# A recurrent chain of four layers: when the preparation for the last layers is done, and in which pieces

## The chip, the cores and the metric

The kernel runs on one NeuronCore of a Trainium2 chip. The metric is the device time of one execution in microseconds (us), the median of several runs. A NeuronCore has a matrix engine (TensorE, in profiles PE, its weight loads PEld), two engines for elementwise work (VectorE or DVE, ScalarE or ACT), a programmable one (GpSimd or POOL) and a synchronisation engine (SyncE or SP) that issues most DMA transfers here. Each engine takes its own instructions strictly in the order in which the program gives them, and they wait for each other through semaphores. TensorE writes to PSUM[...]; the other engines read results from there.

## The reference

Four residual layers follow one another on x of shape (4, 1024, 512), with a conditioning vector per batch row:

```
x = x + rnn(x)            # h = tanh(x_t Wx + h Wh), 1024 steps in order
x = x + ssm(x)            # convolution, projections, a scan with decay, projection
x = x + lstm(x)           # gates = x_t Wx2 + h Wh2, 1024 steps in order
x = x + adaptive(x, cond) # x @ layer[b]; layer[b] = base + A_b B_b^T
```

`A_b` and `B_b` (512 by 8 each) come from the conditioning vector: layer norm, a hidden layer with Gelu, and a product with the big matrix w2. They don't depend on x, so they are prepared while the recurrences run. Everything is in fp32; the LSTM's recurrent product is done with three bf16 parts of Wh2 and three of h.

## The kernel before

Time is cut into 32 chunks of 32 steps (`TC`, `NCHUNK`). The RNN runs `LEAD` = 56 steps ahead of the LSTM. `do_pass(c)` is one chunk of LSTM steps, with the RNN steps 56 further on; the passes c = -2 (24 steps) and c = -1 (32 steps) have RNN steps alone and are called the lead here. Its steps are counted 0 to 55; step 24 is the first of pass -1. One RNN step is 16 matrix products on TensorE (`rnn_mm`, line 337, 32 records since an fp32 product is two instructions), a transpose and an addition on VectorE (`rnn_pre`, lines 352 and 353) and a tanh on ScalarE (`rnn_h`, line 356). One LSTM step is 96 products (line 369) in two halves A and Bh, each followed by a transpose, a sum, gates, products, cell, tanh, h and two splits of h.

The order of every engine's instructions is written out by hand (`manual_schedule`). Within a step there are three places for other work: "pe", after the LSTM's products and ahead of the RNN's; "gap", ahead of the tanh of half Bh; and "end", after the RNN's tanh. Jobs of a chunk (`ssm_jobs`, `input_jobs`, `project0`, `adapt_jobs`) are lists of (step, place, function). In chunk 0 there is no adaptive layer of an earlier chunk, so that the "pe" place of steps 17, 19, 21 and 23 is empty; that of 29 and 31 is empty in all chunks. In the lead, `keep_busy` adds eight products without use per step up to step 31.

The preparation is a separate list, `early`: a function registered with `at(c, t, f)` or `at_step(i, f)` (lead step i) runs at the very end of that step. It holds, in this order of steps:

- `split_wh2` (269 to 283): 16 pieces of Wh2 (128 by 512 each), loaded into the later place of `layer`, are split into three bf16 parts. Each piece takes four instructions, alternately on ScalarE and VectorE: part 0 (276), remainder `left` (277), part 1 (280), part 2 (281). The first two of a piece are in one step and the last two in the next, steps 5 to 21.
- `load_w1`, `load_w2`, `load_base` at steps 10, 14 and 18, and 21: SyncE loads into the places of `layer` that the split has read. w2 comes in 32 pieces of 512 KB through four buffers.
- `fold_conv` (20), `adapt_center` (23), `adapt_norm` (25), `adapt_bias` (26, 27), `double_g` (27 to 30, one ScalarE instruction each), `adapt_hidden` (31: 16 products, transpose, addition, Gelu).
- `adapt_w2` (583 to 595): 16 groups of 16 products on two pieces of w2 each, with a copy by ScalarE and the loads of the two pieces that come two groups later. Six groups are in the lead, at steps 35, 38, ... 50, and ten in chunk 0, at steps 1, 3, ... 19.
- `adapt_gather` (597): eight small DMAs from GpSimd for each half, at steps 3 and 19 of chunk 0.
- `base_identity` (628): 16 VectorE additions of 32 by 32 that add twice the identity to the base layer, at step 21 of chunk 0.
- `adapt_sum` (619), at steps 22 and 23.
- `adapt_layer` (622 to 626): 16 times one product of 8 by 128 and 8 by 512 (two TensorE instructions, into a bank of PSUM) and one VectorE addition of 128 by 512, at steps 24 of chunk 0 to 12 of chunk 1. The 8 rows of batch row b lie at partition 32 b.

Banks come from `bank`; the tag "fill" has two and serves the projections, `adapt_w2` and `adapt_layer`, in turn.

For each chunk `adapt_jobs` adds the LSTM's output to x (696), multiplies with `layer` (703), copies the result by ScalarE (710) and writes it out with four DMAs (712), during the next chunk. For the last chunk the same is called after the last step (line 827).

Of the kernel before, what the change touches and what calls it, by code (L numbers as in the profile page):

```python
# [8 lines left out]
F32 = mybir.dt.float32  # L9
BF16 = mybir.dt.bfloat16  # L10
AF = mybir.ActivationFunctionType
ALU = mybir.AluOpType
# [26 lines left out]
def cond_resid_kernel(ctx: ExitStack, tc: tile.TileContext, a: dict, out: bass.AP):  # L39
# [145 lines left out]
    def upper(x):  # L185

        return x.bitcast(BF16)[..., 1::2]
# [81 lines left out]
    def split_wh2(k, g):  # L269

        w, scale, cols = layer[:, k, g], 1.0 if g == 3 else 0.5, slice(g * D, (g + 1) * D)
        part = [x[:, k, cols] for x in wh2]
        left = xw2[1][:, 2 + g % 2].rearrange("p c t b -> p (c t b)")

        def first():
            nc.scalar.activation(part[0], upper(w), AF.Copy, scale=scale)
            nc.vector.scalar_tensor_tensor(left, w, scale, part[0], ALU.mult, ALU.subtract)

        def second():
            nc.scalar.copy(part[1], upper(left))  # L280
            nc.vector.tensor_tensor(part[2], left, part[1], ALU.subtract)

        return first, second


    def bank(name, shape, tag="fill", bufs=2):
        return psum.tile(shape, F32, name=name, tag=tag, bufs=bufs)
# [331 lines left out]
    def adapt_sum(half):  # L619
        nc.vector.tensor_add(turned[half], turned[half], plain(raw[half]))  # L620

    def adapt_layer(b, k):
        r = slice(32 * b, 32 * b + RANK)
        pl = bank("pl", [P, D])
        nc.tensor.matmul(pl, xt[0][r, k * P : (k + 1) * P], xt[1][r], start=True, stop=True)  # L625
        nc.vector.tensor_add(layer[:, b, k, :], base[:, k, :], pl)

    def base_identity():

        for c in range(KC):  # L630
            for j in range(4):
                n0 = P * j + CT * c
                q = slice(CT * j, CT * (j + 1))
                nc.vector.scalar_tensor_tensor(
                    base[q, c, n0 : n0 + CT], ident[q, q], 2.0, base[q, c, n0 : n0 + CT],
                    ALU.mult, ALU.add,
                )


    early = {}  # L640

    def at(c, t, f):
        early.setdefault((c, t), []).append(f)
# [8 lines left out]
    late = None  # L652
    for n in range(4 * KC):
        first, second = split_wh2((1, 0, 2, 3)[n // 4], n % 4)
        if late:
            at_step(5 + n, late)
        at_step(5 + n, first)
        late = second
    at_step(21, late)

    at_step(10, load_w1)
# [4 lines left out]
    at_step(23, adapt_center)  # L666
    at_step(25, adapt_norm)
    for half in range(2):
        at_step(26 + half, lambda half=half: adapt_bias(half))
    at_step(26, lambda: nc.scalar.activation(b2[:, 3], b2[:, 3], AF.Copy, scale=2.0))  # L670
    for k in range(KC):
        at_step(27 + k, lambda k=k: double_g(k))
    at_step(31, adapt_hidden)
    NPRE = 12
    for j in range(0, NW2, 2):
        f = lambda j=j: adapt_w2(j)
        if j < NPRE:
            at_step(35 + 3 * j // 2, f)
        else:
            at(0, j - NPRE + 1, f)  # L680
        if j % (NW2 // 2) == NW2 // 2 - 2:
            at(0, j - NPRE + 1, lambda half=j // (NW2 // 2): adapt_gather(half))
    at(0, 21, base_identity)
    for half in range(2):
        at(0, 22 + half, lambda half=half: adapt_sum(half))
    for n in range(B * KC):
        c, t = divmod(24 + 4 * n // 3, TC)
        at(c, t, lambda n=n: adapt_layer(n % B, n // B))


    def adapt_jobs(c, dst):
        x3 = work.tile([P, KC, B, TC], F32, name="x3", tag="x3")
        ps = bank("ada", [P, D], tag="ada", bufs=1)

        def add(m):
            nc.vector.scalar_tensor_tensor(  # L696
                x3[:, m].rearrange("p b t -> p t b"), h2[c % 2][:, m, :, 0], 0.5, x2[c % 2][:, m],
                ALU.mult, ALU.add,
            )

        def mm(k):
            for b in range(B):
                nc.tensor.matmul(  # L703
                    ps[TC * b : TC * (b + 1), :], x3[:, k, b, :], layer[:, b, k, :],
                    start=(k == 0), stop=(k == KC - 1),
                )

        def end():
            x4 = work.tile([P, D], F32, name="x4", tag="x4")
            nc.scalar.copy(x4, ps)  # L710
            for b in range(B):
                nc.sync.dma_start(out=dst(b), in_=x4[TC * b : TC * (b + 1), :])

        jobs = [((0, 1, 2, 6)[m], ("end", "gap")[m // 3], lambda m=m: add(m)) for m in range(KC)]
        jobs += [(17 + 2 * k, "pe", lambda k=k: mm(k)) for k in range(KC)]
        return jobs + [(23, "end", end)]


    def input_jobs(c, n, steps, turns):
# [14 lines left out]
        ]  # L734


    def do_pass(c, first=0, src=None, dst=None):

        lstm = c >= 0
        jobs = []  # L740
        if dst is not None:
            jobs += adapt_jobs(c - 1, dst)
        if -1 <= c < NCHUNK - 1:
            jobs += ssm_jobs(c + 1)
            jobs += input_jobs(
                c + 1, 0, range(25, 29), ((28, "end"), (29, "gap"), (29, "end"), (30, "gap"))
            )
        if src is not None:
            jobs.append((9, "end", lambda: load_x(c + 4, src)))
        if c + 3 < NCHUNK:  # L750
            for m in range(KC):
                mm, end = project0(c + 3, m)
                t = (18, 20, 22, 30)[m]
                jobs += [(t, "pe", mm), (t, "end", end)]
        if lstm:
# [64 lines left out]
    for c in range(-1, NCHUNK):  # L820
        if c == 0:
            for m in range(2):
                lstm_input(0, 0, m)
        do_pass(c, src=a["xT"][c + 4] if c + 4 < NCHUNK else None, dst=dst(c - 1) if c > 0 else None)
    assert not early
    prep_ctx.close()
    for _, _, f in adapt_jobs(NCHUNK - 1, dst(NCHUNK - 1)):
        f()


# [56 lines left out]
```

## Time and profile before

The median of three runs is 4768.19 us (4766.73 to 4770.69). The profiled execution took 4770.03 us, of which 4768.2 us lie between its first and last instruction (the span); the granted TensorE clock was 0.999 of full speed on average.

| stage | from, to (us of the span) | length |
|---|---|---|
| loads and first projection, to the end of RNN step 0 | 0 to 19.4 | 19.4 |
| lead, steps 1 to 23 | 19.4 to 83.2 | 63.8 |
| lead, steps 24 to 55 | 83.2 to 157.4 | 74.2 |
| chunk 0 | 157.4 to 320.0 | 162.6 |
| chunk 1 | 320.0 to 473.3 | 153.3 |
| chunks 2 to 30 | 473.3 to 4614.8 | 142.8 each on average |
| chunk 31 | 4614.8 to 4757.3 | 142.5 |
| last adaptive layer and end | 4757.3 to 4768.2 | 10.9 |

A step of the lead ends here with the tanh on line 356, an LSTM step with the second addition on line 415. The page gives the busy time and share of each engine, the granted clock and DMA traffic in slices of the span, and the chain of waits: from the last instruction back to what released it, step by step. Groups of instructions have their line, engine, operation, output and inputs, shape and mean duration. Windows give the same busy times for a stretch of the span. In timelines, "[0.79 <-ACT wh L280]" after an instruction means that its engine had been idle for 0.79 us before it, until line 280 on ScalarE was done; "issue" means that it waited for nothing that the profile shows.

### The profile page before, as it was taken

Reading aid. Unit: us, or ns where it says so; the run is one execution under the profiler, and the core shown is the slowest. Engines: PE = TensorE matmul, PEld = TensorE weight load, DVE = VectorE, ACT = ScalarE, POOL = GpSimd, SP = SyncE. Lnnn points to the kernel's source line nnn. Section 1 sums busy time; section 2 is a strip of 40 time slices with the busy share of each in tenths; the row PEclk is TensorE's granted clock in tenths of the full one; section 3 lists DMA queues with packets and bytes.
Section 4 is the critical chain, followed back from the end, with each engine's and each line's share of the span. In section 5 each row is a group of like instructions: output and inputs, shape, how many; then the busy total and the mean of one; then the engine's idle time right before and its main releaser. Section 6 shows DMA issues by size and latency. Waiting matters only on the chain.

```text
span 4768.2 us, 320158 instructions
## 1 busy us (share of the span) xinstructions
PE 4608.4 (97%) x146784; PEld 3524.3 (74%) x146784; DVE 3867.3 (81%) x18001; ACT 1493.9 (31%) x7645; POOL 45.6 (1%) x80
## 2 busy tenths in 40 slices
PE   7999999999999999999999999999999999999976
PEld 5767777777777777777777777777777777777654
DVE  3688888888888888888888888888888888888876
ACT  2223333333333333333333333333333333333322
POOL 3000000000000000000000000000000000000000
PEclk9999999999999999999999999999999999999999
DMA  6300000000000000000000000000000000000000
GB/s 148 112 13 9 9 7 9 9 7 9 9 7 9 9 7 9 9 7 9 9 7 9 9 7 9 9 7 9 9 7 9 9 7 9 9 5 7 6 5 7
DMA packets 38266, 67.36 MB, mean 14 GB/s; under 512 B 8609, under 2 KB 25505, under 8 KB 35889
## 3 DMA queue, kind: packets, MB, share of 16 engines
q1 hardware_dynamic: 34064, 46.68, 3.6%
q8 instruction: 1147, 18.79, 1.6%
q14 instruction: 207, 1.69, 0.1%
q0 software_dynamic: 1696, 0.19, 0.0%
q10 hardware_dynamic: 1152, 0.01, 0.0%
HBM read 38.34 MB, written 8.39 MB: 10 GB/s over the span
## 4 chain that ended last, share of the span: by engine, by line
PE 94%; DVE 4%; DMA 1%; issue 1%; ACT 0%; SPq 0%; ACTq 0%; DVEq 0%
PE acc L369 59%; PE acc L337 18%; PE proj L318 9%; PE pb L292 3%; PE proj L292 2%; PE ada L703 2%; DVE tt L386 1%; DVE gc L391 1%; DVE h L191 1%; PE ssm_out L292 1%; DMA layer<-in_w_dram 1%; DVE h L415 0%; DVE prod L402 0%; DVE gc L407 0%; PE pl L625 0%
## 5 line engine op out<-in xcount | busy, mean ns | idle before, releaser
L369 PE MATMUL acc<-wh,h 128*12 128x256 bf16 x98304 | 2868.0, 273 | 118.4 <-DVE h L191 115.2
L369 PEld LDWEIGHTS <-h 128*12 128x12 bf16 x98304 | 2262.6, 87 | 676.8 <-DVE h L191 360.6
L386 DVE STREAM_TRANSPOSE tt<-acc 128x256 f32<-128x256 f32 x2048 | 920.9, 450 | 429.2 <-PE acc L369 301.4
L337 PEld LDWEIGHTS acc<-wh,h 128*4 128x4 f32 x32768 | 805.4, 87 | 510.0 <-issue 214.8
L337 PE MATMUL acc<-wh,h 128*4 128x128 f32 x32768 | 1086.1, 273 | 18.1 <-ACT h L356 11.0
L398 ACT ACTIVATE gc<-gc 128x32 f32<-128x32 f32 x2048 | 469.8, 229 | 1279.1 <-DVE gc L391 1192.2
L391 DVE TENSOR_REDUCE gc<-tt 128x32 f32<-128x128 f32 x2048 | 775.4, 379 | 35.3
L191 DVE TENSOR_TENSOR h<-h 128x8 f32<-128x8 f32 (+1 forms) x4098 | 680.5, 166 | 104.8
L412 ACT ACTIVATE th<-gc 128x8 f32<-128x8 f32 x2048 | 427.7, 209 | 830.1 <-DVE gc L407 830.1
L356 ACT ACTIVATE h<-pre 128x16 f32<-128x16 f32 x1024 | 221.2, 216 | 1132.2 <-DVE pre L353 1132.2
L318 PE MATMUL proj<-wx,x 128*32 128x512 f32 x4096 | 529.1, 592 | 1.1 <-DVE x L507 1.1
L415 DVE SCALAR_TENSOR_TENSOR h<-gc,th 128x8 f32<-128x8 f32 x2048 | 341.8, 167 | 144.6 <-ACT th L412 134.7
L407 DVE SCALAR_TENSOR_TENSOR gc<-prod 128x8 f32<-128x8 f32 x2048 | 342.0, 167 | 35.5
L352 DVE STREAM_TRANSPOSE tt<-acc 128x128 f32<-128x128 f32 x1024 | 316.0, 309 | 61.8 <-PE acc L337 61.6
L375 ACT COPY tt<-xw 128x32 f32<-128x32 f32 x2048 | 327.8, 207 | 0.0
L402 DVE SCALAR_TENSOR_TENSOR prod<-gc 128x16 f32<-128x16 f32 x2048 | 314.3, 153 | 0.0
L353 DVE TENSOR_TENSOR pre<-xw,tt 128x16 f32<-128x16 f32 x1024 | 179.3, 175 | 38.0 <-DVE tt L352 0.5
L292 PE MATMUL proj<-xin,wx 128*32 128x128 f32 x4096 | 137.9, 278 | 11.1 <-DMA wx<-in_Wx_dram 11.1
L703 PE MATMUL ada<-layer,x 128*32 128x512 f32 x1024 | 133.9, 599 | 3.0 <-DVE x L696 3.0
L292 PE MATMUL pb<-x,wp 128*32 128x128 f32 x4096 | 134.4, 273 | 0.0
L292 PEld LDWEIGHTS proj<-xin,wx 128*32 128x32 f32 x4096 | 117.5, 112 | 14.9 <-DMA wh<-in_Wh_dram 11.1
L318 PEld LDWEIGHTS proj<-wx,x 128*32 128x32 f32 x4096 | 118.3, 110 | 6.6 <-DVE x L507 1.4
(118 smaller groups left out, 1168.8 us busy)
## 6 DMA issues: line engine op xcount, KB each, us to landing
layer<-in_w2T_dram SPq DMA_DIRECT2D x32, 512.0 KB, 4.5
xin<-in_xT_dram SPq DMA_DIRECT2D x128, 64.0 KB, 2.4
out_dram<-x SPq DMA_DIRECT2D x128, 64.0 KB, 2.0
layer<-in_Wh_dram SPq DMA_DIRECT2D x16, 256.0 KB, 9.9
wx<-in_Wx_dram SPq DMA_DIRECT2D x4, 1024.0 KB, 15.6
wx<-in_Wx_dram SPq DMA_DIRECT2D x4, 256.0 KB, 4.6
wh<-in_Wh_dram SPq DMA_DIRECT2D x4, 256.0 KB, 7.2
layer<-in_w_dram SPq DMA_DIRECT2D x4, 256.0 KB, 23.9
```

Source lines behind the costliest of these rows:

```text
L191: nc.vector.tensor_tensor(h[:, :, n], h[:, :, n - 1], upper(h[:, :, n - 1]), ALU.subtract)
L292: nc.tensor.matmul(dst[CT * j : CT * (j + 1)], columns(j), x, start=first, stop=final)
L318: nc.tensor.matmul(ps[CT * j : CT * (j + 1), :], tok, w[:, j], start=(k == 0), stop=(k == KC - 1))
L337: nc.tensor.matmul(acc0[CT * j : CT * j + B, :], h[:, k, (t - 1) % TC, :], wh0[:, k, j * P : (j + 1) * P], start=(k == 0), stop=(k == KC - 1),
L369: nc.tensor.matmul(acc2[mh][CT * j : CT * j + NP * B, :], parts, w[:, :, n0 : n0 + 2 * CT], start=(k == 0 and n == 0), stop=(k == KC - 1 a ...
L375: nc.scalar.copy(tt2[m][t % 2][:, :, :, :B], xw2[c % 2][:, :, 2 * m : 2 * m + 2, t, :])
L386: nc.vector.transpose(self.tt[:, :, :, B:].rearrange("p g c b -> p (g c) b"), acc2[self.m])
L391: nc.vector.tensor_reduce(self.gc[:, :4].rearrange("p g c b -> p (g c) b"), self.tt[:, :, :, : (1 + NP) * B].rearrange("p g c (s b) -> p ( ...
L398: nc.scalar.activation(self.gc[:, :4], self.gc[:, :4], AF.Tanh, scale=0.5)
L407: nc.vector.scalar_tensor_tensor(self.c, self.prod[:, 1], 0.5, self.prod[:, 0], ALU.mult, ALU.add)
L412: nc.scalar.activation(self.th, self.c, AF.Tanh, scale=0.5)
L415: nc.vector.scalar_tensor_tensor(self.out[:, :, 0], self.gc[:, 2], 1.0, self.th, ALU.add, ALU.mult)
```

## The change

1. `split_wh2` gives its four instructions singly, and each is put at its own step: piece i starts at step 5 + i, its four instructions at steps 5 + i, 6 + i, 7 + i and 8 + i. The remainders have four buffers. Within a step the order is: part 2 of piece i - 3 and remainder of piece i - 1 (VectorE), part 1 of piece i - 2 and part 0 of piece i (ScalarE). The last is at step 23. The loads and `adapt_center` that follow move by one or two steps.
2. `adapt_hidden` goes from step 31 to 29, `double_g` to 30, 32, 34 and 36.
3. The w2 groups: eight in the lead (steps 31, 33, 35, 39, 41, 45, 47, 51), eight in chunk 0 (steps 1, 3, ... 15). The first gather is at step 51 of the lead, the second at step 15 of chunk 0; the sums at steps 6 and 18 of chunk 0.
4. The identity is added at steps 40, 42, 44 and 46 of the lead, four additions each.
5. `adapt_layer` does two batch rows at once: two products, one after the other in TensorE's order, then one addition; the second addition is put at the end of the next step (`later`). The pairs are at steps 19, 21, 23, 29 and 31 of chunk 0 and 10, 12 and 14 of chunk 1.
6. In the last chunk, the output for steps 0 to 27 is added to x during steps 28 and 29; after the last step come additions for the four others, and the products in two halves of 256 columns. The first half is copied by ScalarE and written out from SyncE, the second copied by VectorE and written out from ScalarE's queue.

```diff
-        left = xw2[1][:, 2 + g % 2].rearrange("p c t b -> p (c t b)")
+        left = xw2[g % 2][:, 2 + g // 2].rearrange("p c t b -> p (c t b)")
+        return (
+            lambda: nc.scalar.activation(part[0], upper(w), AF.Copy, scale=scale),
+            lambda: nc.vector.scalar_tensor_tensor(left, w, scale, part[0], ALU.mult, ALU.subtract),
+            lambda: nc.scalar.copy(part[1], upper(left)),
+            lambda: nc.vector.tensor_tensor(part[2], left, part[1], ALU.subtract),
+        )
...
-    def adapt_layer(b, k):
-        r = slice(32 * b, 32 * b + RANK)
-        pl = bank("pl", [P, D])
-        nc.tensor.matmul(pl, xt[0][r, k * P : (k + 1) * P], xt[1][r], start=True, stop=True)
-        nc.vector.tensor_add(layer[:, b, k, :], base[:, k, :], pl)
+    def adapt_layer(n):
+        def add(b, k, pl):
+            nc.vector.tensor_add(layer[:, b, k, :], base[:, k, :], pl)
+        pls = []
+        for x in (n, n + 1):
+            b, k = x % B, x // B
+            r = slice(32 * b, 32 * b + RANK)
+            pl = bank("pl", [P, D])
+            nc.tensor.matmul(pl, xt[0][r, k * P : (k + 1) * P], xt[1][r], start=True, stop=True)
+            pls.append((b, k, pl))
+        add(*pls[0])
+        later.append(lambda: add(*pls[1]))
...
+    stages = [split_wh2((1, 0, 2, 3)[n // 4], n % 4) for n in range(4 * KC)]
+    for i in range(4 * KC + 3):
+        for n, f in ((i - 3, 3), (i - 1, 1), (i - 2, 2), (i, 0)):
+            if 0 <= n < 4 * KC:
+                at_step(5 + i, stages[n][f])
+    at_step(11, load_w1)
     for j in range(W2_BUFS):
-        at_step((14, 18)[j // 2], lambda j=j: load_w2(j))
-    at_step(21, load_base)
+        at_step((15, 19)[j // 2], lambda j=j: load_w2(j))
+    at_step(23, load_base)
...
+    at_step(29, adapt_hidden)
     for k in range(KC):
+        at_step(30 + 2 * k, lambda k=k: double_g(k))
+        at_step(40 + 2 * k, lambda k=k: base_identity(k))
+    for j in range(0, NW2 // 2, 2):
+        at_step((31, 33, 35, 39, 41, 45, 47, 51)[j // 2], lambda j=j: adapt_w2(j))
+        at(0, j + 1, lambda j=j: adapt_w2(NW2 // 2 + j))
+    at_step(51, lambda: adapt_gather(0))
+    at(0, NW2 // 2 - 1, lambda: adapt_gather(1))
+    at(0, 6, lambda: adapt_sum(0))
+    at(0, 18, lambda: adapt_sum(1))
+    for n, (c, t) in enumerate(((0, 19), (0, 21), (0, 23), (0, 29), (0, 31), (1, 10), (1, 12), (1, 14))):
+        at(c, t, lambda n=n: adapt_layer(2 * n))
...
+    def last_adapt(c, dst):
+        x3, x4 = adapt_tile("x3"), adapt_tile("x4")
+        ready = TC - 4
+        def rest():
+            for m in range(KC):
+                adapt_add(c, m, x3, ready)
+            for n, (tag, copy, dma) in enumerate(
+                (("ada", nc.scalar.copy, nc.sync), ("po", nc.vector.tensor_copy, nc.scalar))
+            ):
+                cols = slice(n * D // 2, (n + 1) * D // 2)
+                ps = bank("ada", [P, D // 2], tag=tag, bufs=1)
+                for k in range(KC):
+                    adapt_mm(k, x3, ps, cols)
+                copy(x4[:, cols], ps)
+                for b in range(B):
+                    dma.dma_start(out=dst(b)[:, cols], in_=x4[TC * b : TC * (b + 1), cols])
+        return [(28 + m // 2, ("gap", "end")[m % 2], lambda m=m: adapt_add(c, m, x3, 0, ready)) for m in range(KC)], rest
...
             do(t, "end")
+            while later:
+                later.pop()()
             for f in early.pop((c, t), ()):
                 f()
+        if last is not None:
+            rest()
```

More of the change, by code (lines that the diff above doesn't have):

```diff
@@ L272, in split_wh2 @@
         part = [x[:, k, cols] for x in wh2]
-        left = xw2[1][:, 2 + g % 2].rearrange("p c t b -> p (c t b)")
[L275 to L283, printed above, removed]
+        left = xw2[g % 2][:, 2 + g // 2].rearrange("p c t b -> p (c t b)")
[5 more added lines that the diff above has]
+        )
     def bank(name, shape, tag="fill", bufs=2):
@@ L620, in adapt_sum, with base_identity @@
         nc.vector.tensor_add(turned[half], turned[half], plain(raw[half]))
-    def adapt_layer(b, k):
-        r = slice(32 * b, 32 * b + RANK)
-        pl = bank("pl", [P, D])
-        nc.tensor.matmul(pl, xt[0][r, k * P : (k + 1) * P], xt[1][r], start=True, stop=True)
-        nc.vector.tensor_add(layer[:, b, k, :], base[:, k, :], pl)
[L628 to L640, printed above, removed]
+    def adapt_layer(n):
[10 more added lines that the diff above has]
+        later.append(lambda: add(*pls[1]))
+    def base_identity(c):
+        for j in range(4):
+            n0 = P * j + CT * c
+            q = slice(CT * j, CT * (j + 1))
+            nc.vector.scalar_tensor_tensor(
+                base[q, c, n0 : n0 + CT], ident[q, q], 2.0, base[q, c, n0 : n0 + CT],
+                ALU.mult, ALU.add,
+            )
+    early, later = {}, []
     def at(c, t, f):
@@ L651, in cond_resid_kernel @@
         at_step(1 + n // 2, f)
[L652 to L661, printed above, removed]
+    stages = [split_wh2((1, 0, 2, 3)[n // 4], n % 4) for n in range(4 * KC)]
[4 more added lines that the diff above has]
+    at_step(11, load_w1)
     for j in range(W2_BUFS):
-        at_step((14, 18)[j // 2], lambda j=j: load_w2(j))
-    at_step(21, load_base)
+        at_step((15, 19)[j // 2], lambda j=j: load_w2(j))
+    at_step(23, load_base)
     at_step(20, fold_conv)
-    at_step(23, adapt_center)
+    at_step(24, adapt_center)
     at_step(25, adapt_norm)
@@ L670, in cond_resid_kernel @@
     at_step(26, lambda: nc.scalar.activation(b2[:, 3], b2[:, 3], AF.Copy, scale=2.0))
+    at_step(29, adapt_hidden)
     for k in range(KC):
[L672 to L688, printed above, removed]
-    def adapt_jobs(c, dst):
[L692 to L706, printed above, removed]
+        at_step(30 + 2 * k, lambda k=k: double_g(k))
@@ new lines, in adapt_add, with adapt_mm @@
+    def adapt_add(c, m, x3, t0=0, t1=TC):
+        nc.vector.scalar_tensor_tensor(
+            x3[:, m, :, t0:t1].rearrange("p b t -> p t b"), h2[c % 2][:, m, t0:t1, 0], 0.5, x2[c % 2][:, m, t0:t1],
+            ALU.mult, ALU.add,
+        )
+    def adapt_mm(k, x3, ps, cols=slice(0, D)):
+        for b in range(B):
+            nc.tensor.matmul(
+                ps[TC * b : TC * (b + 1), :], x3[:, k, b, :], layer[:, b, k, cols],
+                start=(k == 0), stop=(k == KC - 1),
+            )
@@ L708, in end, with adapt_tile @@
+    def adapt_tile(name):
+        return work.tile([P, KC, B, TC] if name == "x3" else [P, D], F32, name=name, tag=name)
+    def adapt_jobs(c, dst):
+        x3, ps = adapt_tile("x3"), bank("ada", [P, D], tag="ada", bufs=1)
         def end():
-            x4 = work.tile([P, D], F32, name="x4", tag="x4")
+            x4 = adapt_tile("x4")
             nc.scalar.copy(x4, ps)
@@ L712, in end @@
                 nc.sync.dma_start(out=dst(b), in_=x4[TC * b : TC * (b + 1), :])
-        jobs = [((0, 1, 2, 6)[m], ("end", "gap")[m // 3], lambda m=m: add(m)) for m in range(KC)]
-        jobs += [(17 + 2 * k, "pe", lambda k=k: mm(k)) for k in range(KC)]
+        jobs = [((0, 1, 2, 6)[m], ("end", "gap")[m // 3], lambda m=m: adapt_add(c, m, x3)) for m in range(KC)]
+        jobs += [(17 + 2 * k, "pe", lambda k=k: adapt_mm(k, x3, ps)) for k in range(KC)]
         return jobs + [(23, "end", end)]
+    def last_adapt(c, dst):
[12 more added lines that the diff above has]
+                copy(x4[:, cols], ps)
+                for b in range(B):
+                    dma.dma_start(out=dst(b)[:, cols], in_=x4[TC * b : TC * (b + 1), cols])
+        return [(28 + m // 2, ("gap", "end")[m % 2], lambda m=m: adapt_add(c, m, x3, 0, ready)) for m in range(KC)], rest
     def input_jobs(c, n, steps, turns):
@@ L734, in input_jobs, with do_pass @@
         ]
-    def do_pass(c, first=0, src=None, dst=None):
+    def do_pass(c, first=0, src=None, dst=None, last=None):
         lstm = c >= 0
@@ L742, in do_pass @@
             jobs += adapt_jobs(c - 1, dst)
+        if c == NCHUNK - 1:
+            more, rest = last_adapt(c, last)
+            jobs += more
         if -1 <= c < NCHUNK - 1:
@@ L823, in cond_resid_kernel @@
                 lstm_input(0, 0, m)
-        do_pass(c, src=a["xT"][c + 4] if c + 4 < NCHUNK else None, dst=dst(c - 1) if c > 0 else None)
+        do_pass(
+            c, src=a["xT"][c + 4] if c + 4 < NCHUNK else None, dst=dst(c - 1) if c > 0 else None,
+            last=dst(c) if c == NCHUNK - 1 else None,
+        )
     assert not early
     prep_ctx.close()
-    for _, _, f in adapt_jobs(NCHUNK - 1, dst(NCHUNK - 1)):
-        f()
 def kernel(**inputs):
```

## The prediction

> **What bounds the kernel now.** I read the page first (busy shares, the chain by engine, the costliest group), then the windows by stage, the chain of waits and the timelines of the stages that the change touches.
>
> ```profile
> span 4768.2 us, 320158 instructions
> PE 94%; DVE 4%; DMA 1%; issue 1%; ACT 0%; SPq 0%; ACTq 0%; DVEq 0%
> q8 instruction: 1147, 18.79, 1.6%
> ```
>
> ```profile
> 32.00:72.00 40.00, 32.42 (x632) 18.27 (x627) 23.70 (x64) 17.72 (x44) 10.55 (x13) 0.93 0.96 209
> 320.00:402.00 82.00, 82.00 (x2307) 57.53 (x2300) 63.74 (x282) 21.61 (x114) 0.00 (x0) 1.00 0.03 7
> 473.00:616.00 143.00, 141.43 (x4576) 109.00 (x4572) 119.49 (x560) 45.87 (x238) 0.00 (x0) 1.00 0.03 8
> ```
>
> The windows' columns: stretch, length, busy time of TensorE, its weight loads, VectorE, ScalarE and GpSimd (with counts), clock, DMA share, GB/s. TensorE carries the chain; in the second window, the steps with layer products, it is busy all 82.00 us. The last window is a steady chunk: 32 steps of 4.46 us, which the change doesn't touch (chunks 2 to 30, each 142.5 to 143.2 us by the ends of line 415). What it touches is the lead (56 RNN steps up to 157.4 us), chunk 0 (162.6 us), half of chunk 1 (153.3 us) and the 10.9 us after the last step. So the stake is the 20 us that chunk 0 and the 10.6 us that chunk 1 take above 142.7, some of the lead, and a little at the end. The chain there:
>
> ```profile
> 269.36 0.19 DVE layer L634
> ...
> 272.00 4.49 PE acc L369 x96
> ...
> 282.92 1.05 PE pl L625 x2
> 283.97 2.73 PE acc L369 x96
> 286.69 0.86 PE proj L318 x8
> 287.55 0.87 PE acc L337 x32
> 288.42 1.05 PE pl L625 x2
> ```
>
> Each layer product (pl) stands between two steps and lengthens one by its 1.05 us. The 16 identity additions in one step end at 269.4, TensorE idles, and its next LSTM products take 4.49 instead of 2.75 us. The timelines of VectorE, TensorE and of the end:
>
> ```profile
> 266.43 3.12 DVE L634 SCALAR_TENSOR_TENSOR layer<-ident,layer 32x32 f32<-32x32 f32 x16
> ```
>
> ```profile
> 48.97 0.69 DVE L281 TENSOR_TENSOR wh<-xw,wh 128x512 bf16<-128x512 f32 x1 [0.79 <-ACT wh L280]
> 49.57 0.68 DVE L277 SCALAR_TENSOR_TENSOR xw<-layer,wh 128x512 f32<-128x512 f32 x1
> 50.18 0.31 DVE L352 STREAM_TRANSPOSE tt<-acc 128x128 f32<-128x128 f32 x1
> ```
>
> ```profile
> 53.83 0.50 PE L337 MATMUL acc<-wh,h 128*4 128x128 f32 x10 [2.00 <-issue]
> ...
> 63.31 0.62 PE L292 MATMUL idle<-xin 128*32 128x512 f32 x2 [1.82 <-issue]
> ```
>
> ```profile
> 4758.14 5.25 PE L703 MATMUL ada<-layer,x 128*32 128x512 f32 x32 [2.98 <-DVE x L696]
> ...
> 4763.45 0.58 ACT L710 COPY x<-ada 128x512 f32<-128x512 f32 x1 [6.34 <-PE ada L703]
> 4764.06 1.71 SPq L712 DMA_DIRECT2D out_dram<-x  x4
> ```
>
> In the lead VectorE waits for ScalarE inside the split, and the RNN's transpose queues behind (2.52 us a step against 2.02 undisturbed). But TensorE also stops with no releaser ("issue").
>
> [...] No row-tiled pair is in this trace; the column-tiled groups do run four abreast (32 records of 128 columns in 0.87 us). [...] Page section 3 agrees (18.79 MB in 1147 packets, 16 KB each), and so do the stops: counted in the trace, they come after TensorE records 705, 961, 1473, 1729 and 1985, multiples of 256 apart. From entry into a block to the start of the next took 8.1 to 9.5 us where data fill the DMA engines (32 to 72 us, busy 0.96).
>
> **The change, part by part** (against the profiled execution: span 4768.2, its time 4770.03, the median of the runs 4768.19; a difference in span is carried over to the median).
>
> *Split in four stages.* The same 64 instructions, now none waiting for the other engine inside a step. VectorE per step: transpose to sum 0.35, sum 0.09, two splits 0.61 each: 1.66 of 2.02. Eleven of the steps 6 to 19 would shed 0.5 each, 5.5; those with an RNN projection (10, 12, 14) don't, since TensorE has 3 x 0.87 = 2.61 there. But the blocks run late: a block of 256 records is 3.2 steps, 8.1 us at 2.52 and 6.5 at 2.02, and its successor takes 8.1 to 9.5 anyway. Only the block that started at 39.41 got its successor in time; following the steps through it and through 71.97 to 79, I find 0.4 + 0.3 gained. Taken: -0.7; bounds 0 and -5.5.
>
> *Hidden layer at step 29, w2 groups in the lead.* Before, hidden at 31 with the first taps cost 2.5 over two steps. Moved: its 0.87 of products starts 0.3 after the RNN's, then Gelu behind a table load (1.28, the measured row) holds the tanh: 1.6. A w2 group (0.87) is free where the next step has no other TensorE job, and costs 0.6 where it has one, since 0.96 of idleness takes only one. Before: 6 groups, dear ahead of 36, 42 and 51 (0.60 + 0.67 + 0.58 = 1.85). After: 8 groups; the one ahead of 32 costs 1.46 with the taps and the warming products of step 31; those ahead of 34, 36, 42, 46 and 52 some 0.6 each, of 40 0.4, of 48 nothing (that step waits for the scan): 3.5. Change: 1.6 + 1.46 + 3.5 - 2.5 - 1.85 = +2.2. Loads have 4 steps or more (8 us) against the 5.8 of the slowest pair. double_g (0.61 of ScalarE) lies in its 1.7 us gaps: nothing.
>
> *Identity in four steps of the lead.* 4 x 0.195 = 0.78 of VectorE at steps 40, 42, 44, 46; its idle time before the transposes covers it at 42 and 46, short by 0.3 and 0.2 at 40 and 44: +0.5.
>
> *w2 in chunk 0.* Ten groups become eight. Of the ten, those at steps 17 and 19 were free (step lengths 4.45 and 4.54: no other TensorE job there in chunk 0), the others cost 0.75, and stay. Block stops there were 3.9 us; with 6 pairs of loads for 8, -0.8. In the lead, 8 loads for 6: +0.5. The first gathered sum (0.68) at step 6: +0.15.
>
> *Layer products, identity, second sum.* Before, above 4.46: steps 19 to 31 of chunk 0 10.45 (identity and the cold clock 5), chunk 1 10.6; together 21.05. After: a pair costs TensorE one 1.05 if it overlaps. At 19, 21, 23, 29 and 31 the slot before the RNN's products is empty, so 0.2 is left (measured: the product at step 29 made it 4.66); at 10, 12, 14 of chunk 1 the slot is full: 3 x 1.07 = 3.2. VectorE becomes the bound at 19 to 25: it is busy 3.8 to 4.1 of 4.46, and each of these steps gets one operation of 0.68; the second sum before, at such a step, made it 4.98. Six times 0.45 and 0.3: 3.0 (bounds 1.2 and 4.5). Steps 29 and 31: 0.3 each. The second addition is queued behind everything of its step, and the bank it holds is not needed until the next pair: nothing. Sum 6.9, so -14.1. If the pairs ran one after the other: 2.1 each, 7.3 more.
>
> *Last chunk.* Four additions of 0.17 instead of 0.39 let the products start 0.2 earlier; their sum (5.25, of it 3.3 at half clock) is the same, half of it copied and sent while the other runs; the last copy is 256 columns (0.4 for 0.58), its four issues (1.7) follow as before. -0.7, and +0.2 for two additions of 0.36 in the gap of steps 28 and 29: -0.5. [...]
>
> Sum: -0.7 + 2.2 + 0.5 - 0.8 + 0.5 + 0.15 - 14.1 - 0.5 = -12.75. Forecast 4768.2 - 12.8 = **4755.4 us**, alone 4751 to 4759.5.
>
> **Rivals.** A: the blocks arrive earlier than I think and the split yields its 5.5: 4750.6. [...] against it, the five stops. B: the pairs don't overlap (a wait on TensorE's own semaphore, or the two fp32 records in order): 4755.4 + 7.3 = 4762.7. For it, both records of a pl today run in sequence; against it, column tiles of the same kind run abreast. C, the other side: block stops in steps 31 to 54, where w2 traffic grows by a third. There a block is run in 4.2 us; if its successor took the 8.7 of the early lead, each stop costs 4.5. From the third on the gain is gone; six, 27, give 4782. Against it, six pairs of loads caused no stop of more than 0.1 us there.
>
> **Chances.** Forecast 0.62, A 0.20, B 0.15, C 0.03. A measurement tells 0.2% (9.5 us, below 4758.65) from no change. Faster: 0.9 of the forecast, all of A, a tenth of B: 0.77; slower: C, 0.03; same 0.20. Range 4749 to 4762: A's lower end to most of B.
>
> **What would show it.** Pairs: four pl records within 1.1 us, and 1.07 above 4.46 at steps 10, 12, 14 of chunk 1. Identity: no 4.49 us of LSTM products, full clock from 265 to 320. Split: no wait of VectorE on lines 280 and 276, but stops as long or longer at the same records. Lead: LSTM starts 2 to 3 us later than 157.4. The forecast is wrong if chunk 0 isn't shorter by 5 to 10 us, or if the lead moves by more than 4 either way.

## The result, and the profile after

The changed kernel takes 4752.6 us, the median of seven runs (4747.13 to 4754.05), against 4768.19 us before (4764.6 to 4772.8 in seven runs). The ratio is 0.9965, with a 95% interval of 0.9953 to 0.9977. The forecast was 4755.4 us.

The profiled execution of the changed kernel took 4751.75 us, close to the median. First the page: the span and the chain's shares by engine.

```profile
span 4750.0 us, 320243 instructions
PE 94%; DVE 5%; issue 1%; ACT 0%; DMA 0%; ACTq 0%; SPq 0%; DVEq 0%
```

VectorE's share of the chain has gone from 4 to 5%, while TensorE keeps 94%. The stages, by the ends of RNN steps and LSTM steps in the two traces:

| stage | before | after | difference | forecast |
|---|---|---|---|---|
| lead, to the end of RNN step 55 | 157.40 | 160.51 | +3.1 | +2.5 |
| chunks 0 and 1 | 315.91 | 299.70 | -16.2 | -14.75 |
| chunks 2 to 30 | 4141.52 | 4138.26 | -3.3 | 0 |
| chunk 31 | 142.47 | 142.41 | -0.1 | +0.2 |
| after the last h | 10.85 | 9.08 | -1.8 | -0.7 |

The windows of the changed kernel follow, with the columns explained ahead of the prediction. The first is the early lead, the second the stretch of chunk 0 in which the identity was added before, the third the layer products of chunk 1, the last a steady chunk.

```profile
32.00:72.00 40.00, 31.53 (x580) 17.62 (x576) 20.55 (x56) 15.56 (x40) 12.53 (x16) 0.87 0.98 212
265.00:320.00 55.00, 54.62 (x1688) 40.51 (x1680) 48.61 (x219) 16.55 (x88) 0.00 (x0) 1.00 0.02 4
320.00:402.00 82.00, 81.91 (x2537) 61.23 (x2528) 68.55 (x311) 24.54 (x129) 0.00 (x0) 1.00 0.03 8
466.00:609.00 143.00, 141.43 (x4580) 108.96 (x4576) 119.64 (x560) 45.80 (x237) 0.00 (x0) 1.00 0.03 8
```

The second window before, which the prediction didn't show, was:

```profile
265.00:320.00 55.00, 50.63 (x1436) 36.35 (x1428) 44.98 (x201) 13.91 (x74) 0.00 (x0) 0.97 0.02 4
```

In the first window TensorE ran 580 records instead of 632, at a clock of 0.87 instead of 0.93: the early lead did not get faster. In the second and third it is nearly always busy and at full clock, and they hold more records (1688 instead of 1436, 2537 instead of 2307): the same time contains more steps.

The lines of the changed kernel differ from those before: 276 is the remainder of a split, 288 a helper that records several kinds of products, 333 and 348 the products and the transpose of the RNN, 365 the products of the LSTM, 629 the layer products, 691 and 698 the additions and products of the last layer. The chain of waits shows a pair of layer products as one piece:

```profile
275.21 0.87 PE acc L333 x32
276.08 1.06 PE pl L629 x4
277.14 2.75 PE acc L365 x96
```

Four records take 1.06 us, where two took 1.05. The pairs run side by side.

The timelines of VectorE and of TensorE in the early lead:

```profile
45.81 0.68 DVE L276 SCALAR_TENSOR_TENSOR xw<-layer,wh 128x512 f32<-128x512 f32 x1
46.72 0.32 DVE L348 STREAM_TRANSPOSE tt<-acc 128x128 f32<-128x128 f32 x1 [0.22 <-PE acc L333]
```

```profile
38.11 0.28 PE L333 MATMUL acc<-wh,h 128*4 128x128 f32 x2 [2.66 <-issue]
53.79 0.81 PE L333 MATMUL acc<-wh,h 128*4 128x128 f32 x10 [2.82 <-issue]
63.83 1.06 PE L288 MATMUL idle<-xin 128*32 128x512 f32 x2 [2.66 <-issue]
```

VectorE no longer waits for ScalarE: it is ready for the transpose before TensorE is done. What it gained TensorE loses in the stops with no releaser. In both traces those of the early lead stand multiples of 256 records (products and weight loads) apart; the 256 records from one such place to the next are called a block here. Measured from the start of a block's last record to the start of the next block's first (the timelines give the idle time alone, which is less), the five stops that the prediction listed were 2.80, 0.60, 2.27, 2.41 and 0.70 us before and are 1.49, 2.93, 3.09, 3.25 and 0.36 after: three are longer and two shorter, 2.3 us more in all.

That these stops are waits for instructions is a reading of the DMA records. Queue q8, whose kind the page gives as "instruction", carried 1147 packets of 16 KB, and 1147 times 256 is 293632, the number of TensorE's records in the changed kernel. Between 22 and 330 us of the traces before and after, TensorE was idle 14 times for more than 0.3 us with no releaser. In 13 of them it went on 1.2 to 1.7 us after a packet of q8 had landed; after record 1473 of the changed kernel the packet landed at 52.25 and TensorE went on at 53.79. The fourteenth lies at the first products of the hidden layer in the changed kernel (99.04, 0.40 us).

### The profile page after: what moved, and what is told of

Read it like the earlier page. It is cut to its first block, busy times and chain, and to the rows that moved or that the text cites. A ratio compares the mean times of both kernels' runs of the same rounds, so it can differ in the third digit from the quotient of the medians.

```text
span 4750.0 us, 320243 instructions
## 1 busy us (share of the span) xinstructions
PE 4593.9 (97%) x146816; PEld 3521.8 (74%) x146816; DVE 3865.3 (81%) x18006; ACT 1494.6 (31%) x7645; POOL 46.7 (1%) x80
## 3 DMA queue, kind: packets, MB, share of 16 engines
q8 instruction: 1147, 18.79, 1.6%
## 4 chain that ended last, share of the span: by engine, by line
PE 94%; DVE 5%; issue 1%; ACT 0%; DMA 0%; ACTq 0%; SPq 0%; DVEq 0%
PE acc L365 59%; PE acc L333 18%; PE proj L314 9%; PE pb L288 3%; PE proj L288 2%; PE ada L698 2%; DVE tt L382 1%; DVE gc L387 1%; DVE h L191 1%; PE ssm_out L288 1%; PE idle L288 0%; DVE h L411 0%; DVE prod L398 0%; DVE gc L403 0%; PE pp L585 0%
## 5 line engine op out<-in xcount | busy, mean ns | idle before, releaser
L698 PE MATMUL ada<-layer,x 128*32 128x512 f32 (+1 forms) x1056 | 132.0, 579 | 2.8 <-DVE x L691 2.8
```

## Experiments

Each is compared with the kernel before, run on the same chip at the same time, whose median was 4768.88 us beside experiments 1 to 4, 4770.25 beside 5 to 8 and 4771.45 beside 9; so ratios compare better than times. "Stop" means the time from the start of the last record of a block of 256 TensorE instructions to the start of the first of the next.

**1. The split alone.** The kernel before, with only the four-stage split (and the one or two steps by which its loads and `adapt_center` move).

```diff
+    stages = [split_wh2((1, 0, 2, 3)[n // 4], n % 4) for n in range(4 * KC)]
+    for i in range(4 * KC + 3):
+        for n, f in ((i - 3, 3), (i - 1, 1), (i - 2, 2), (i, 0)):
+            if 0 <= n < 4 * KC:
+                at_step(5 + i, stages[n][f])
```

> The kernel before with the four-stage split alone (w1, w2 and base loads and adapt_center at the steps that go with it). Theory of the blocks (TensorE's next 256 instructions arrive 8 to 9.5 us after the current block was entered, as long as the data loads fill the DMA engines): steps that aren't stopped take 2.0 us, but the stops after records 961, 1473 and 1729 grow to about 3 us, so that step 23 ends within 1 us of the 83.2 us of before, and the whole is 4767 to 4769 us. Rival (the wait inside the split was what the lead paid for): no VectorE wait, step 23 ends 5 us earlier, whole 4763 us.

Measured: 4766.86 us, ratio 1.0001 (0.9993 to 1.001). Step 23 ends at 83.65, before at 83.18; the lead at 157.82. TensorE's timeline:

```profile
39.42 0.38 PE L333 MATMUL acc<-wh,h 128*4 128x128 f32 x2 [2.93 <-issue]
54.30 0.50 PE L333 MATMUL acc<-wh,h 128*4 128x128 f32 x10 [2.20 <-issue]
63.51 1.07 PE L288 MATMUL idle<-xin 128*32 128x512 f32 x2 [3.22 <-issue]
```

The stops after records 961, 1473 and 1729 are 3.20, 2.47 and 3.81 us here. The split by itself gains nothing that could be told; the stops grow as the steps shrink.

**2. Only the loads spread.** The kernel before, with the early loads of Wx2, w1, the first w2 pieces and base started later and apart. A memset of one column holds each load back until VectorE reaches that step. Nothing of the computation is left out.

```diff
+    def load_wx2(j):
+        q = slice(CT * j, CT * (j + 1))
+        hold(wx2[q, 0, 0:1])
+        nc.sync.dma_start(out=wx2[q], in_=a["Wx2"].rearrange("(j c q) n -> j q c n", j=4, c=KC)[j])
...
-    at_step(10, load_w1)
+    for j, i in enumerate((9, 15, 20, 25)):
+        at_step(i, lambda j=j: load_wx2(j))
+    at_step(12, load_w1)
     for j in range(W2_BUFS):
-        at_step((14, 18)[j // 2], lambda j=j: load_w2(j))
-    at_step(21, load_base)
+        at_step((18, 23)[j // 2], lambda j=j: load_w2(j))
+    at_step(28, load_base)
```

> The kernel before with its two-stage split, but the loads of Wx2, w1, w2 and base spread over steps 9 to 28 of the lead (each held back by a one-column memset on VectorE at its step), so that about 1 MB is under way at a time. Theory of the blocks: [...] the stops after 1473 and 1729 go, and the half clock after them; step 23 ends 4 to 6 us earlier than 83.2, the whole 4762 to 4764 us. Rival (a stop every 256 records whatever the traffic): stops unchanged, whole 4768 us.

**3. Both.** The edits of 1 and 2 together.

> Both: the four-stage split and the loads spread out. Theory of the blocks: with the stops gone the split's gain shows at last, 0.5 us at each step without a projection: step 23 ends 7 to 10 us earlier than 83.2 and 3 to 4 us earlier than with the loads spread alone; whole 4758 to 4761 us. Rival (the split saves nothing by itself): as with the loads spread alone.

Measured:

| | time, us | ratio | step 23 ends | lead ends |
|---|---|---|---|---|
| split | 4766.86 | 1.0001 (0.9993 to 1.001) | 83.65 | 157.82 |
| loads spread | 4764.48 | 0.9990 (0.9981 to 0.9999) | 80.83 | 155.03 |
| both | 4758.68 | 0.9978 (0.9971 to 0.9986) | 75.39 | 149.53 |

The windows of the early lead, first with the loads spread, then with both:

```profile
32.00:72.00 40.00, 32.03 (x688) 18.61 (x684) 25.16 (x73) 18.71 (x47) 10.90 (x14) 0.96 0.63 138
```

```profile
32.00:72.00 40.00, 36.86 (x799) 23.00 (x799) 27.66 (x79) 20.59 (x51) 16.26 (x22) 0.96 0.72 168
```

With the loads spread the stops at records 1473, 1729 and 1985 are gone (0.01 us and less), in both kernels; those at 705 and 961, in the stretch where Wh2 itself is loaded, stay at 2.7 to 3.0 us. With the loads spread alone step 23 ends only 2.4 us earlier, where 4 to 6 were expected. Steps 13 to 19 save 4.5 us, but the stop after record 961 was 2.69 us in this execution and 0.60 in the profile before, which costs steps 8 to 10 some 2.9. The steps that no stop holds are as long as before, since with the old split VectorE still waits for ScalarE:

```profile
48.49 0.69 DVE L294 TENSOR_TENSOR wh<-xw,wh 128x512 bf16<-128x512 f32 x1 [1.04 <-ACT wh L293]
```

(Lines are higher by 13 there.) Only with both does step 23 end 7.8 us earlier. Of these, 5.4 come from the split (80.83 to 75.39), more than the 3 to 4 expected here and close to the 5.5 that the prediction gave to a split with blocks in time. Whichever of the two limits is later sets the time, so each hides the gain from removing the other. The medians agree in kind, with a smaller excess over the sum: 2.0 us less than the kernel before for the split alone, 4.4 for the loads alone, 10.2 for both.

**4. Pairs that can't overlap.** The changed kernel, where a pair takes two k of one batch row, so that the operands of both products lie on the same eight partitions.

```diff
-        for x in (n, n + 1):
-            b, k = x % B, x // B
+        for x in (0, 1):
+            b, k = n // 2 % B, 2 * (n // 2 // B) + x
```

> The changed kernel, but a pair of layer products is two k of one batch row instead of two batch rows of one k: the same products, additions and banks[...]. Theory (row groups overlap): the pair takes 2.1 us instead of 1.06; +1.05 at steps 11, 13 and 15 of chunk 1, +1 at 30 and 32 (0), +0.7 to 0.9 at 20, 22, 24 of chunk 0: +7 us, whole 4759 to 4761 us. Rival (the gain came from the empty slots and the spread additions, not from overlap): chunk 1 unchanged at 146.3 us, whole 4752.6 us.

Measured: 4760.22 us, ratio 0.9983 (0.9976 to 0.9990); chunks 0 and 1 take 155.86 and 149.78 us, 5.9 more than the changed kernel's. The chain:

```profile
366.43 1.91 PE pl L629 x4
```

Two products one after the other take 1.91, so the overlap is worth 0.85 for each pair, where TensorE is the limit: steps 11, 13 and 15 of chunk 1 go from 5.54 to 6.39. The prediction took 1.05. The pairs account for 5.3 of the 5.9; the rest is stops in chunk 0.

**5. w2 groups at even steps.** The changed kernel with another list of steps for the lead's eight groups.

```diff
-        at_step((31, 33, 35, 39, 41, 45, 47, 51)[j // 2], lambda j=j: adapt_w2(j))
+        at_step((32, 34, 36, 38, 40, 42, 44, 46)[j // 2], lambda j=j: adapt_w2(j))
```

> The changed kernel with the lead's eight w2 groups behind steps 32, 34, ... 46 instead of 31, 33, 35, 39, 41, 45, 47, 51. Theory of the shared gap: a group (0.87 us of TensorE) and the next step's own TensorE job share 0.96 us of idle time, so each odd place costs; behind an even step the next one has no such job. The steps 32, 34, 36, 42, 46, 52 and 53, which measured 3.40, 2.69, 2.62, 2.69, 2.61, 2.61 and 2.37, fall to about 2.0 to 2.1: lead 157.0 (from 160.5), whole 4749 (from 4752.6). Rival: the longer steps come from late instructions or from the w2 loads themselves, whose number is the same: lead 160 to 161, whole 4752 to 4753.

Measured: 4754.34 us, ratio 0.9967 (0.9954 to 0.9979), so no gain over the changed kernel's 0.9965 that could be told; 4749 had been expected. The lead is shorter by 3.1 us (157.43), but 1.3 of it lie before step 24, where the two programs are the same and only the stops differ. In the steps 32 to 55, the groups' moves save 2.8 (steps 34, 36 and 52 fall by 0.6 to 0.7 each, 40, 42 and 46 by 0.2 to 0.3, step 32 by 0.2), and 0.9 is lost at step 38, where TensorE stops with no releaser:

```profile
116.95 0.52 PE L288 MATMUL pb<-x,wp 128*32 128x128 f32 x9 [0.84 <-issue]
```

Both theories hold in part: the shared gap is what the groups cost, and when the steps get shorter the stop takes a third of it back. Chunk 0 is longer by 1.1 too, at block ends. Step 32, where a group and the conv's first taps had been priced at 1.46 together, still takes 3.19 without the group: the taps wait for VectorE, and the group cost 0.2.

```profile
103.54 1.08 PE L288 MATMUL pb<-x,wp 128*32 128x128 f32 x32 [0.46 <-DVE x L430]
```

**6. Even steps and spread loads.** The edits of 2 and 5 on the changed kernel.

> As the run with even places, and with the loads of Wx2, w1, the first w2 pieces and base spread over steps 9 to 28 as in the spread runs. If late instruction blocks are what kept the four-stage split from paying, the lead loses the 8.3 us by which the split with spread loads was shorter than the split alone: lead 148.7, whole 4741. Rival: the w1, w2 or base pieces that now start later come late, so hidden (step 29) or the first groups (32, 34) wait for them: a step of 4 us or more among 30 to 36, lead 152 or more, whole above 4744.

Measured: 4745.99 us, ratio 0.9950 (0.9937 to 0.9962). The lead ends at 149.63, close to the 148.7 expected. The whole misses its 4741 because that started from the 4749 expected of experiment 5; against what experiment 5 measured it is 8.4 less, and the spread loads had been given 8.3. No load came late in a way that held hidden (its step is 3.69, in the changed kernel 3.68), but step 36 takes 3.41 with a stop of 1.6 us in it.

**7. More of w2 in the lead.** In addition, eleven groups in the lead and five in chunk 0, the two gathers (now at step 48 of the lead and 9 of chunk 0) and the second sum earlier, pairs from step 17 on.

```diff
+            at_step((32, 34, 36, 38, 40, 42, 44, 46, 47, 52, 54)[j // 2], lambda j=j: adapt_w2(j))
...
-    at(0, 18, lambda: adapt_sum(1))
-    for n, (c, t) in enumerate(((0, 19), (0, 21), (0, 23), (0, 29), (0, 31), (1, 10), (1, 12), (1, 14))):
+    at(0, 14, lambda: adapt_sum(1))
+    for n, (c, t) in enumerate(((0, 17), (0, 19), (0, 21), (0, 23), (0, 29), (0, 31), (1, 10), (1, 12))):
```

> As even_spread, and eleven w2 groups in the lead (also behind 47, 52 and 54) with five left in chunk 0, the second sum at step 14, pairs of layer products from step 17 on and two left in chunk 1. Each group in chunk 0 measured 0.75 above 4.46, a pair in chunk 1 1.08, one at step 19 to 23 0.2 to 0.4: 3 x 0.75 + 0.8 = 3.0 less than even_spread, whole 4738. Rival: the added loads in steps 44 to 55 come late or delay TensorE's instructions: lead longer by 2 to 4 than in even_spread, whole 4740 to 4743.

Measured: 4740.38 us, ratio 0.9936 (0.9922 to 0.9950): the fastest of all, 5.6 below the run before it. The lead ends at 152.26, 2.6 later than there, all of it before step 24, where the programs are the same and the stops differ; steps 24 to 55 take 76.0 and 76.1, so three more groups cost nothing. Chunk 0 takes 148.84 (153.90) and chunk 1 145.15 (146.38), 6.3 less together. That is more than the 3.0 expected, because most block stops of chunk 0 vanish with its w2 loads: in steps 1 to 16 they come to 0.6 us instead of 3.2. The same stretch of the span, in experiment 6 and here (share and GB/s of the DMA at the end of each line):

```profile
198.00:238.00 40.00, 37.24 (x1250) 31.43 (x1245) 27.12 (x129) 11.86 (x63) 4.49 (x8) 1.00 0.18 58
```

```profile
198.00:238.00 40.00, 39.93 (x1311) 31.91 (x1304) 32.29 (x153) 12.82 (x67) 3.92 (x7) 1.00 0.03 6
```

**8. The old end.** The changed kernel with the last adaptive layer in one piece of 512 columns after the last step, as before.

```diff
-        do_pass(
-            c, src=a["xT"][c + 4] if c + 4 < NCHUNK else None, dst=dst(c - 1) if c > 0 else None,
-            last=dst(c) if c == NCHUNK - 1 else None,
-        )
+        do_pass(c, src=a["xT"][c + 4] if c + 4 < NCHUNK else None, dst=dst(c - 1) if c > 0 else None)
...
+    for _, _, f in adapt_jobs(NCHUNK - 1, dst(NCHUNK - 1)):
+        f()
```

> The changed kernel with the old end: the last chunk's adaptive layer in one 512-column half after the last step, one copy, four stores. If the column halves themselves save time, the tail after the last h grows from 9.08 to 10.8 or more whatever the clock (whole +1.7, 4754.3). If the gain came from TensorE's clock being full there by chance, the tail is 9.3 where the products run at full clock and 10.9 where they run at half: whole +0.2 or +1.8, and the clock's slice at the end tells which.

Measured: 4755.23 us, ratio 0.9969 (0.9956 to 0.9981). The tail is 9.25 us, with the products in 3.64. The changed kernel's tail of 9.08 has them in 3.66; the run of experiment 5, with the new end, has 5.35 and a tail of 10.76. The products of the last layer, in the changed kernel and in experiment 5:

```profile
4741.53 3.66 PE L698 MATMUL ada<-layer,x 128*32 128x256 f32 x64 [2.79 <-DVE x L691]
```

```profile
4742.44 5.35 PE L698 MATMUL ada<-layer,x 128*32 128x256 f32 x64 [2.80 <-DVE x L691]
```

The idle time before is the same. Over all traces, the old end has tails of 9.25 (products at full clock) and 10.65 to 10.94 (half clock for a while), the new end 9.08 and 10.76 to 10.86. So the halves are worth 0.1 to 0.2 us, and the 1.7 is whether TensorE falls to half clock after its last idle time.

The traces show what went with it. In the profiles before and after, the changes of the granted clock up to the last product lie a whole number of 3.41 us apart (in the changed kernel at 39.56, 42.97, 53.21, 56.63, 63.45 and 66.87, before at 30.55, 33.96, 54.44, 57.85, 272.89, 276.31, 4758.01 and 4761.42), on a grid that starts elsewhere in each of the two. Of the grid's windows at full clock between 15 us and the last product, the seven in which TensorE was idle for 1.96 us or more were followed by one at half clock, and none of those with 1.82 or less was, as the traces model idle time. Why the clock falls is not shown. The last idle time of the changed kernel (2.79 us) is cut by the grid into 0.98 and 1.81 us, that of experiment 5 into 0.71 and 2.09. The windows that hold the second parts, and for experiment 5 the next one with its clock of 0.50:

```profile
4739.72:4743.13 3.41, 1.60 (x32) 1.21 (x36) 1.55 (x13) 0.46 (x3) 0.00 (x0) 1.00 0.00 0
```

```profile
4740.35:4743.76 3.41, 1.32 (x25) 1.00 (x29) 1.82 (x14) 0.65 (x3) 0.00 (x0) 1.00 0.00 0
4743.76:4747.17 3.41, 3.41 (x37) 2.13 (x33) 0.00 (x0) 0.37 (x1) 0.00 (x0) 0.50 0.11 26
```

So the 1.7 us are luck, by where the last idle time lies on the grid: two of the eleven traces have their last products at full clock, one with each end.

**9. The identity in one step again.** The changed kernel, with the sixteen additions behind step 17 of chunk 0.

```diff
-        at_step(40 + 2 * k, lambda k=k: base_identity(k))
+        at(0, 17, lambda k=k: base_identity(k))
```

> The changed kernel with the sixteen identity additions together behind step 17 of chunk 0, as one block on VectorE, instead of four at each of the lead's steps 40, 42, 44 and 46. Theory of the cold clock: VectorE's 3.12 us hold the next LSTM step by some 2.7, TensorE idles about 2.8 and drops to half clock, so step 18 takes 7.2 (from 4.47) and step 19 6.3 (from 4.97), with LSTM products of over 4 us and a clock below 1 in that stretch: chunk 0 longer by 4.0, whole 4756.5. Rival: only the additions' own time above VectorE's slack counts: step 18 longer by 2 to 2.7, step 19 unchanged, clock 1.00, whole 4755. The lead's steps 40 to 46 tell what the identity cost there: the prediction said 0.5 in all; the trace of the changed kernel suggests nothing.

Measured: 4758.35 us, ratio 0.9974 (0.9965 to 0.9984). Step 18 takes 7.03 (4.47) and step 19 6.12 (4.97), together 3.7 more. (Chunk 0 is longer by 6.0 in all; the rest is mostly block stops in steps 7 to 11, 2.4 us more than in the profile of the changed kernel.) TensorE's timeline:

```profile
249.23 2.80 PE L365 MATMUL acc<-wh,h 128*12 128x256 bf16 x96 [0.78 <-DVE h L191]
...
256.27 4.46 PE L365 MATMUL acc<-wh,h 128*12 128x256 bf16 x96 [2.50 <-DVE h L191]
```

The stall is 2.6 and half clock adds 1.1: the first theory, with both sizes a little smaller. The slow products followed 2.50 us of idleness here, with a mean granted clock of 0.91 from 256 to 275 us, and 2.80 in the kernel before, with 0.50 from 272.89 to 276.31. The lead's steps 40 to 46 are what they were with the additions in them (2.62, 1.95, 2.69, 2.02, 1.95, 2.02, 2.62), so the identity costs nothing there.

## Why the prediction was right, step by step

**Split.** Forecast -0.7, its rival -5.5. Step 23 ended 0.5 later, in the split alone as in the changed kernel. The reason given, blocks that take 8.1 to 9.5 us anyway, held (ahead of the stops after records 961, 1473, 1729 and 1985 they took 8.1 to 10.0 in the changed kernel); following the steps through two of the blocks was too fine a calculation, since in the six programs with the new split and the old loads step 23 ended between 82.3 and 84.0. Of the signs named, the longer stops came at three of the five records. That rival A was a true potential and not a fact of this kernel is shown by experiment 3: with the blocks in time the split gives its 5.4.

**Hidden and w2 in the lead.** Forecast +2.2; the steps 30 to 52 give +2.3 by the two traces (hidden 1.66 instead of 1.6; the groups ahead of steps 34, 40 and 46 cost 0.67, 0.55 and 0.59; those ahead of 36 and 42 had been paid before). A further 0.35 at step 53 was not foreseen. It stays there when no group is near it (experiment 5) and is absent in experiment 9, which has the same groups; its cause wasn't sought. The +0.5 for stops in this part did not come: there was none in the profile after. So the lead's +3.1 is 0.5 (split), 2.3, 0 (identity), 0 (stops) and 0.35, where -0.7, 2.2, 0.5 and 0.5 had been taken: its closeness to +2.5 owes something to misses that cancel.

**Identity.** Forecast +0.5 in the lead; it costs 0 (experiment 9). The slack before the transposes had been read too small. The gain in chunk 0 was priced at 5 with half clock; put back alone, it costs 3.7. That the 4.49 us of products before ran partly at half clock is shown by the granted clock, 1.00 from 269.48 to 272.89 and 0.50 in the 3.41 us after.

**w2 and block stops in chunk 0.** The eight groups cost 0.74 each, as taken (0.75). By the lengths of steps 1 to 18 (above 4.46, or 5.21 with a group) the stops came to 4.0 us in the profile before and 2.9 after, a gain of 1.1 for the 0.8 taken. But experiments 4, 5, 8 and 9, with the same eight groups, have 3.5 to 5.3, and 1 to 3, with the ten groups of before, 4.2 to 6.2: the difference is no larger than the scatter of single executions.

**Layer products.** Forecast 6.9 above 4.46 us a step (the terms as given add up to 6.8), measured 5.8: steps 11, 13 and 15 of chunk 1, which follow the pairs behind 10, 12 and 14, 3 x 1.08 (taken 1.07); steps 19 to 25 of chunk 0 2.2 where 3.0 had been taken, the mis-sized term; the pairs at steps 29 and 31 0.2 each instead of 0.3. VectorE did become the bound for steps 19 to 25, and the chain shows its transposes and reductions there, but the six additions of 0.67 cost 0.1 to 0.4 each, 1.7 together, and not 0.45 each, and the second sum 0.5 and not 0.3.

**Tail.** Forecast -0.5 (-0.7 after the last h, +0.2 in the steps before it); measured -1.8 after the last h, of which 0.2 at most is the halves and the rest the luck of the clock (products in 3.66 us at full clock, before in 5.25; experiment 8).

**What isn't the change.** Chunks 2 to 30 are 3.3 us shorter in the profile after. In the trace before, five of these chunks are longer by 0.3 to 0.5, in the trace after two, by 0.2 to 0.3, and the others are shorter by some 0.05; why wasn't sought; the runs of experiments 5 to 9, with the same code in these chunks, have 4140.3 to 4141.0 us there. Together with the tail's clock some 3 to 5 us of the profile's -18.2 come from such differences. Experiment 8 shares all but the end with the changed kernel: its lead differs by +3.1 and its chunks 0 and 1 by -15.0 from before, which with 0.2 for the end is -12.1, near the forecast's -12.75. The medians' -15.6 has an interval of -11.0 to -22.4, which holds this, but can't confirm it to the microsecond.

**Rivals.** That products on different partitions would overlap was not shown before the change; only column tiles ran abreast there (32 records in 0.87 us). A is refuted for this kernel (experiment 1), B for its pairs (the 1.06 us for four records; experiment 4 shows what B would have been: 4760.2 against the 4762.7 worked out). C didn't happen in the changed kernel; stops of 0.3 to 1.1 us at these places in experiment 5, and of up to 1.9 in 6 and 7, show that stops do begin there when the lead's steps get short.

## What to carry to other kernels

Before an engine's waits are pipelined away, look at what TensorE waits for with no releaser. Where these stops lie at equal numbers of instructions, as here at multiples of 256 records, shorter steps can move their time into the stops, as the split alone did (ratio 1.0001): try first to spread the bulk loads that run beside them (0.9990), then to shorten the steps (0.9978 with both). Work that is free inside an engine's idle time stayed free here only where nothing else of that engine stood in the same gap (a w2 group beside another job cost 0.55 to 0.67 us); list each step's jobs and put movable ones in the empty gaps.

## What the runs showed of the hardware

- While loads held the DMA engines at a share of 0.96 (before) and 0.98 (changed kernel) between 32 and 72 us, blocks of 256 TensorE records with a stop behind them took 8.0 to 10.0 us from their start to that of the next (10.0 in the changed kernel, from 53.79 to 63.83), with stops of up to 3.25 us, and TensorE went on 1.2 to 1.7 us after a packet of q8 had landed. With a share of 0.63 to 0.77 (experiments 2, 3 and 6) the three stops of the second half of the early lead vanished; in experiment 7, with 0.73, one came back with 1.05 us. In chunk 0, between 198 and 238 us, TensorE still sat idle with no releaser for 1.34 us in the kernel before (share 0.30) and for 1.08 in experiment 6 (0.18).
- The same early program had different stops from one execution to the next (at record 961: 2.93 us in the changed kernel, 3.20 in experiment 1); step 23 ended between 82.3 and 84.0 us in the six programs that have it.
- Two products of 8 rows by 512 columns in fp32 took 1.06 us with operands on different partitions (changed kernel), and 1.91 on the same ones (experiment 4).
- After idle times of 2.79 and 2.80 us the same products took 3.66 us at full clock in the changed kernel and 5.35 in experiment 5, where the clock was 0.50 from 4743.76 to 4747.17. In the profiles before and after, the clock changed on a grid of 3.41 us; the seven full-clock windows with 1.96 us or more of idleness were followed by half clock, those with 1.82 or less were not (experiment 8).
